# Dealing attention's score pieces by slots of 128 columns, and reading the experts' places three units later

## The chip, the cores and the metric

The kernel runs on one core of one Trainium2 chip. The metric is device time in microseconds of one execution; before the change the median of three runs is 1528.75 us (1524.66 to 1529.18). The profile comes from one further execution of 1526.24 us.

## The reference

Two layers over x of 2 x 2048 tokens with 256 features. What matters here is the attention of the second layer, cut from the reference:

```python
xn = _layernorm(x, axis=-1)
q = heads(xn @ Wq + bq); k = heads(xn @ Wk + bk); v = heads(xn @ Wv + bv)     # 16 heads of 16
slopes = 1.0 / base ** jnp.arange(1, 9)                                        # base = 24 ** (1 / 8)
fwd = slopes * jnp.tril(rel) + jnp.triu(neg, 1)        # heads 0 to 7 look back
bwd = slopes * jnp.triu(-rel) + jnp.tril(neg, -1)      # heads 8 to 15 look ahead
scores = jnp.einsum('bhqd,bhkd->bhqk', q, k) * (1.0 / np.sqrt(hd)) + bias[None]
out = jnp.einsum('bhqk,bhkd->bhqd', softmax(scores), v) ... @ Wf + bf
```

Around it: layer 0 (a gated linear attention and a linear layer with quantised weights), which comes first, and beside and after attention a mixture of 8 experts (hidden size 1024): a Sinkhorn iteration over the router's logits, the two best experts of each token, and their outputs added with their weights.

## The kernel before

The program runs layer 0, then attention, then the experts' blocks. The change touches attention alone, which is lines 1606 to 1980.

**Heads and row groups.** Each head's 16 features are padded to 32 rows, so that four heads fill TensorE's 128 rows. A score matmul uses 32 of them (a row group, `r` 0 to 3), and the four row groups work side by side. `way` is the direction (0 looks back, 1 looks ahead), and each way has two groups of four heads.

**Pieces.** Queries go by tiles of 256 (`QT`), and a step is (batch, way, query tile); a part is a step and one of its groups of heads. For each row group, `pieces_of` (line 1617) lists a part's pieces: one block of 128 keys against up to 256 queries. A piece on the diagonal needs a mask. For a head with a steep slope, far keys weigh nothing, so the outer pieces are narrower: 32, 64, 96 and so on to 256 columns of queries.

**Units.** `_units` (1606) deals the pieces out when the program is built. A unit gives each row group up to 512 columns (`WIDE`), which is one PSUM bank of scores. Pieces are taken in the order of the list; where the next does not fit into what is left of the 512, the largest that fits is taken first, and where none fits a piece is cut. So nearly every unit has exactly 512 columns in every row group, with pieces of any multiple of 32. There are 148 units and 1772 pieces. Their order within a unit goes by the columns that each row group has been given so far (`taken`).

**A unit's work.** `scores` (1825) multiplies each piece, keys as the stationary operand (32 rows x 128 columns), queries as the moving one (line 1831), into the tile `sc`, a PSUM bank for each row group; ScalarE then takes the exponential of each row group's bank into `pt` (line 1837). `keep_only` (1840) cuts the diagonal pieces with a mask, on VectorE, one unit later. `weighted_sums` (1846) multiplies `pt` with the values (128 rows x 32 columns, line 1851) into `o_ps`, two units later (`LATE`). A matmul in full precision is two records of the trace. The `sc` banks come from a pool of six that all small PSUM tiles of the stage share.

**Chores.** Between units stand: the copy of a finished part (`o_sb`), its transposes (`o_tr`, line 1787, and `on_tr`, line 1806) and the output projection (`f_ps`, line 1541); one step of the router (Sinkhorn and the choice of experts) a unit, on VectorE mostly; then the sends of token rows into a table by expert, on GpSimd (line 2208).

**The experts' start.** Counted from the last unit: at 32 (`BEGIN`) the places of the first two blocks are loaded from the table into `at` (line 2257, on SyncE's queue, after all sends) and their weights are gathered on GpSimd. At 14 (`FETCH`) VectorE turns the places into indices and weights (`fetch_rows`, lines 2275 to 2282, three instructions a block), and GpSimd gathers the tokens' rows into `xb` (line 2554, two gathers a block). In the four units after that, one sum each of the first block's weights is formed (`combine`, 2287). At 4 from the end `xb` is transposed (`open_rows`, 2301, into `x_ps`). VectorE's instructions in these functions stand in the order in which they are written.

The order of TensorE's instructions is made by the framework's scheduler from this program; in the built program bursts of scores and bursts of weighted sums alternate, with the chores between.

Of the kernel before, what the change touches and what calls it, by code (L numbers as in the profile page):

```python
# [64 lines left out]
P = 128  # L65
# [14 lines left out]

ORDERS = ((0, 1, 7, 6, 2, 3, 4, 5), (2, 3, 5, 4, 0, 1, 7, 6))
WIDE = 512
CENTER = N // 2
NEG_INF = -1.0e9
NE, FF = 8, 1024
# [14 lines left out]
LIMIT = 16.0  # L100
SHIFT = 48.0
BEGIN = 32
FETCH = 14
LATE = 2
OPEN = 4
KR = HD + 5
# [1499 lines left out]
def _units():  # L1606

    tiles = QT // P

    def pieces_of(way, group, r, qt):


        found = [(qt * 2 + way, 0, QT, P * way), (qt * 2 + 1 - way, P * (1 - way), P, 0)]  # L1620
        slope = _slopes()[PLACES[(2 * way + group) * 4 + r] % (H1 // 2)]
        reach = math.ceil((104 + LIMIT - SHIFT) / slope) + 1
        for j in range(1, tiles * (N // QT - 1 - qt if way else qt) + 1):


            width = min(QT, reach - 1 - P * (j - 1))
            if width > 0:
                width = -(-width // 32) * 32
                kb = qt * tiles + tiles - 1 + j if way else qt * tiles - j
                found.append((kb, QT - width if way else 0, width, None))  # L1630
        return found

    steps = [(b, way, qt) for b in range(B) for way in range(2) for qt in ORDERS[way]]
    parts = [(step, group, n % 2) for n, step in enumerate(steps) for group in range(2)]
    rows = []
    for r in range(4):
        row = deque()
        for n, ((b, way, qt), group, bank) in enumerate(parts):
            row.append((n, deque(pieces_of(way, group, r, qt))))
        rows.append(row)  # L1640
    units = []
    done, begun = [[None] * len(parts) for _ in range(4)], set()
    while any(rows):
        this = len(units)
        left, masks = [deque() for _ in range(4)], []
        for r, row in enumerate(rows):
            at = 0
            while row and at < WIDE:
                n, found = row[0]
                b, way, qt = parts[n][0]  # L1650
                if n >= OPEN and any(d[n - OPEN] is None or d[n - OPEN] == this for d in done):
                    break
                first = (r, n) not in begun
                begun.add((r, n))
                if found[0][0] != qt * 2 + way and found[0][2] > WIDE - at:

                    fits = [m for m, piece in enumerate(found) if piece[2] <= WIDE - at]
                    found.rotate(-max(fits, key=lambda m: found[m][2], default=0))
                kb, q0, width, diagonal = found.popleft()
                now = min(width, WIDE - at)  # L1660
                if now < width:
                    rest = None if diagonal is None else diagonal - now
                    found.appendleft((kb, q0 + now, width - now, rest))
                if not found:
                    done[r][n] = this
                    row.popleft()
                left[r].append((r, *parts[n], kb, q0, q0 + now, at, first, not found))
                if diagonal is not None:
                    m0, m1 = max(diagonal, 0), min(diagonal + P, now)
                    if m0 < m1:  # L1670
                        masks.append((r, parts[n][0][1], at + m0, m1 - m0, m0 - diagonal))
                at += now
        widths = [sum(piece[6] - piece[5] for piece in pieces) for pieces in left]
        taken, pieces = [0] * 4, []
        while any(left):
            r = min((r for r in range(4) if left[r]), key=lambda r: taken[r])
            piece = left[r].popleft()
            taken[r] += piece[6] - piece[5]
            pieces.append(piece)
        ended = [part for n, part in enumerate(parts)  # L1680
                 if all(d[n] is not None for d in done) and max(d[n] for d in done) == this]
        units.append((pieces, widths, masks, ended))
    return units
# [3 lines left out]
def attention(  # L1687
# [137 lines left out]
    def scores(pieces, widths):  # L1825
        pt = p2.tile([P, 4, WIDE], F32, tag="pt", name="pt", bufs=4)
        scs = [ps_m.tile([P, WIDE], F32, tag="mm", name="sc") if width else None for width in widths]
        for r, (b, way, qt), group, bank, kb, q0, q1, at, first, last in pieces:
            rows = slice(r * HR, (r + 1) * HR)
            heads = operands.heads[2 * way + group]  # L1830
            nc.tensor.matmul(  # L1831
                scs[r][:, at : at + q1 - q0], lhsT=heads[rows, 1, kb * P : (kb + 1) * P],
                rhs=heads[rows, 0, qt * QT + q0 : qt * QT + q1], start=True, stop=True,
            )
        for r, width in enumerate(widths):
            if width:
                nc.scalar.activation(pt[:, r, 0:width], scs[r][:, 0:width], AF.Exp)  # L1837
        return pt
# [7 lines left out]
    def weighted_sums(pieces, pt):  # L1846


        for r, (b, way, qt), group, bank, kb, q0, q1, at, first, last in pieces:
# [5 lines left out]
            )  # L1855

    units = _units()

    sums = [ps_o.tile([P, 2 * QT], F32, tag=f"o{n}", name="o_ps") for n in range(2)]
# [84 lines left out]
    for n, (pieces, widths, masks, ended) in enumerate(units):  # L1944
        if n in (len(units) // 4 - 4, len(units) // 4):
            next(bias)
        if n == len(units) - BEGIN:
# [5 lines left out]
            for block in ahead:  # L1953
                block.load_gate_up()
        if n == len(units) - FETCH:
            for block in ahead:
                block.fetch_rows()
        if len(units) - FETCH < n <= len(units) - FETCH + 4:
            ahead[0].combine(0, range(n - len(units) + FETCH - 1, n - len(units) + FETCH))
        pt = scores(pieces, widths)  # L1960
# [668 lines left out]
def _constants():  # L2629
# [15 lines left out]
    c["keepmask"] = np.where(mask == 0, np.float32(3e38), np.float32(0))  # L2645
    c["pos"] = np.stack([np.arange(N) - CENTER, np.ones(N)]).astype(f32)
    sel = np.zeros((P, P), f32)
# [26 lines left out]
def _slopes():  # L2674
    half = H1 // 2
    base = np.float32(24.0 ** (1.0 / half))
    return (np.float32(1.0) / base ** np.arange(1, half + 1, dtype=np.float32)).astype(np.float32)


def _bias_rows():  # L2680
# [3 lines left out]
    low = slopes - high  # L2684
    pos = (np.arange(N) - CENTER).astype(np.float32)
    q, k = np.ones((2, H1, KR - HD, N), np.float32)
# [107 lines left out]
```

## Time and profile before

| what | value |
|---|---|
| median of 3 runs | 1528.75 us (1524.66 to 1529.18) |
| profiled execution | 1526.24 us, span 1524.4 us |
| granted TensorE clock | 0.989 |
| attention, first score to last weighted sum | 430.7 to 842.5 us |
| scores, PE (L1831) | 3544 records, 207.6 us busy |
| weighted sums, PE (L1851) | 3544 records, 163.1 us busy |
| exponentials, ACT (L1837) | 589, 302.8 us busy |
| masks, DVE (`keepmask`) | 568, 121.3 us busy |
| largest terms of the chain | PE h_ps 26%, y_ps 14% (experts); sc 9%, o_ps 7%, f_ps 2% (attention) |

How to read it: busy times are unions, so overlapping instructions of one group count once, while the mean of one counts each whole; PE is the matmul, PEld the weight load beside it. The "idle before" column of a group is the time for which its engine stood still just before these instructions, and what ended that. The share of a window is taken of its length.

### The profile page before, as it was taken

How to read it: one execution, taken by the hardware profiler on the slowest of the kernel's cores; microseconds unless marked ns; L12 is line 12 of the kernel's file. 1: busy time of each engine (PE TensorE's matmuls, PEld its weight loads, DVE VectorE, ACT ScalarE, POOL GpSimd, SP SyncE). 2: the span in 40 equal slices, each digit the busy share in tenths (PEclk: the TensorE clock that was granted, in tenths of full speed). 3: DMA queues.
4: the chain of work that ended last, by engine and by line, in shares of the span. 5: the costliest groups of instructions: out<-in, count | busy, mean ns of one | idle time of the engine just before them, and what ended most of it. 6: DMA issues, size and time to landing. Idle time of an engine off the chain costs nothing.

```text
span 1524.4 us, 35795 instructions
## 1 busy us (share of the span) xinstructions
PE 1466.6 (96%) x14948; PEld 1235.1 (81%) x14948; DVE 1010.1 (66%) x2639; ACT 720.6 (47%) x1400; POOL 539.8 (35%) x449
## 2 busy tenths in 40 slices
PE   7889999999899999999999999999999999999996
PEld 4556766776668888778888799989899998989996
DVE  6787677565458876854356677767666776767663
ACT  5445555454467777767877223323232333223221
POOL 4342222122120000598931144343434544343342
PEclk9999999999999999999999999999999999999998
DMA  7001101410452210340041765575765867666541
GB/s 233 0 14 58 56 30 47 101 57 29 111 135 43 44 49 16 53 85 6 4 183 44 244 211 182 185 254 190 257 234 191 257 197 269 205 220 246 176 100 24
DMA packets 75866, 192.09 MB, mean 126 GB/s; under 512 B 19008, under 2 KB 56640, under 8 KB 63232
## 3 DMA queue, kind: packets, MB, share of 16 engines
q0 software_dynamic: 28256, 144.23, 29.0%
q1 hardware_dynamic: 46336, 44.30, 11.6%
q8 instruction: 120, 1.97, 0.5%
q10 hardware_dynamic: 1104, 1.18, 0.3%
q14 instruction: 50, 0.41, 0.1%
HBM read 157.95 MB, written 32.10 MB: 125 GB/s over the span
## 4 chain that ended last, share of the span: by engine, by line
PE 62%; DVE 2%; issue 0%; ACT 0%; POOL 0%; POOLq 0%; ACTq 0%
PE h_ps L119 26%; PE y_ps L119 14%; PE sc L1831 9%; PE o_ps L1851 7%; PE f_ps L1541 2%; PE h_ps L2477 1%; PE x_ps L119 1%; PE o_tr L1787 1%; DVE pt L119 1%; PE on_tr L1806 0%; PE h_ps L2512 0%; DVE va L119 0%; DVE larger L119 0%; DVE o_sb L119 0%; PE h_ps L2500 0%
## 5 line engine op out<-in xcount | busy, mean ns | idle before, releaser
L1837 ACT ACTIVATE pt<-sc 128x512 f32<-128x512 f32 (+1 forms) x589 | 302.8, 600 | 104.0 <-ACT pt L1837 40.4
L1831 PE MATMUL sc<-qk 32*128 32x256 f32 (+6 forms) x3544 | 207.6, 333 | 3.9 <-issue 2.0
L119 DVE TENSOR_TENSOR larger<-larger,h_ps 128x512 f32<-128x512 f32 x160 | 109.9, 687 | 145.0 <-ACT larger L119 83.6
L1831 PEld LDWEIGHTS sc<-qk 32*128 32x128 f32 x3544 | 176.6, 186 | 33.2 <-issue 18.7
L119 PE MATMUL y_ps<-qk,larger 128*128 128x256 f32 x704 | 173.4, 380 | 0.3 <-DVE larger L119 0.3
L1851 PE MATMUL o_ps<-pt,va 128*32 128x256 f32 (+7 forms) x3544 | 163.1, 312 | 1.8 <-DVE o_sb L119 1.8
L119 ACT COPY larger<-h_ps 128x512 f32<-128x512 f32 x128 | 74.5, 582 | 174.9 <-PE h_ps L119 174.9
L1851 PEld LDWEIGHTS o_ps<-pt,va 128*32 128x32 f32 x3544 | 126.4, 110 | 27.3 <-issue 7.5
L2391 POOL DMA_INDIRECT out<-va,to x64 | 103.9, 1623 | 123.4 <-DVE larger L119 69.7
L119 DVE TENSOR_TENSOR pt<-pt,keepmask 128x128 f32<-128x128 f32 (+3 forms) x568 | 121.3, 272 | 34.3 <-ACT pt L1837 34.0
L2208 POOL DMA_INDIRECT table<-rows,place x64 | 68.0, 1063 | 194.5 <-DVE pt L119 180.2
L119 PEld LDWEIGHTS y_ps<-qk,larger 128*128 128x128 f32 x704 | 124.0, 191 | 12.3 <-DVE larger L119 0.7
L119 PEld LDWEIGHTS h_ps<-va,qk 128*128 128x128 f32 x1024 | 126.6, 192 | 6.7 <-issue 3.1
L119 PE MATMUL h_ps<-va,qk 128*128 128x128 f32 x1024 | 130.6, 276 | 0.3 <-ACT larger L119 0.3
L2554 POOL DMA_INDIRECT xb<-normed,to x64 | 65.6, 1025 | 146.6 <-DVE wt L2282 80.4
L119 ACT ACTIVATE larger<-larger 128x512 f32<-128x512 f32 x64 | 40.4, 632 | 117.8 <-DVE larger L119 117.8
L119 ACT ACTIVATE va<-va 128x512 f32<-128x512 f32 x64 | 40.4, 632 | 103.6 <-DVE va L119 103.3
L119 PE MATMUL y_ps<-larger 128*128 128x256 f32 x320 | 79.0, 380 | 0.0
L119 POOL TENSOR_TENSOR pause<-ones_mat,expo 128x4 f32<-128x4 f32 x64 | 68.5, 1071 | 2.0
L119 ACT COPY va<-h_ps 128x512 f32<-128x512 f32 x64 | 36.9, 576 | 56.2 <-PE h_ps L119 56.2
L119 PE MATMUL h_ps<-larger,qk 128*128 128x128 f32 x512 | 62.8, 276 | 0.0
L119 PEld LDWEIGHTS h_ps<-larger,qk 128*128 128x128 f32 x512 | 59.7, 192 | 2.5 <-issue 2.5
(322 smaller groups left out, 2840.7 us busy)
## 6 DMA issues: line engine op xcount, KB each, us to landing
qk<-qk SPq DMA_DIRECT2D x32, 256.0 KB
qk<-qk SPq DMA_DIRECT2D x64, 128.0 KB
va<-v SPq DMA_DIRECT2D x4, 1208.0 KB
v<-v SPq DMA_DIRECT2D x8, 574.0 KB
normed<-xn SPq DMA_DIRECT2D x8, 512.0 KB
out<-acc SPq DMA_DIRECT2D x8, 512.0 KB
acc<-in_x SPq DMA_DIRECT2D x7, 512.0 KB
table<-rows,place POOLq DMA_INDIRECT x64, 3.0
```

Of the source, the lines that this page charges most:

```text
L119: return lambda *a, **k: self.tc.keep_in_program_order(begin(*a, **k))
L1541: multiply(out[r : r + HR], left[:, r : r + HR], *args, **how)
L1787: nc.tensor.transpose(ps[:, n, :], o_sb[:, n * P : (n + 1) * P], ident)
L1831: nc.tensor.matmul(scs[r][:, at : at + q1 - q0], lhsT=heads[rows, 1, kb * P : (kb + 1) * P], rhs=heads[rows, 0, qt * QT + q0 : qt * QT + q ...
L1837: nc.scalar.activation(pt[:, r, 0:width], scs[r][:, 0:width], AF.Exp)
L1851: nc.tensor.matmul(sums[bank][r * HR : (r + 1) * HR, to + q0 : to + q1], lhsT=values[b, way][:, kb, h * VC : h * VC + HR], rhs=pt[:, r, at ...
L2208: send = self.tc.keep_in_program_order(self.nc.gpsimd.indirect_dma_start(out=self.c.table, in_=self.rows[:, t, :], in_offset=None, out_off ...
L2391: send = e.nc.gpsimd.indirect_dma_start(out=e.out, in_=y[:, c, :], in_offset=None, out_offset=bass.IndirectOffsetOnAxis(ap=self.to[:, c : ...
L2477: self.e.nc.tensor.matmul(ps[rows, :], lhsT=self.xT[:, c * P + r * SB : c * P + (r + 1) * SB], rhs=self.w[:, r, at : at + ST], start=c == ...
L2554: self.nc.gpsimd.indirect_dma_start(out=to, out_offset=None, in_=self.c.normed, in_offset=bass.IndirectOffsetOnAxis(ap=at, axis=0),)
```

## The change

Two things are altered.

A unit's row group still holds at most 512 columns, and now also at most 576 slots (`SLOTS`), where a piece counts as its columns, and as 128 at least. `part` is what could be cut off a piece here, a multiple of 128. A part's first (diagonal) piece is taken whole if it fits and cut to `part` if not. Of the other pieces the widest that fits is taken; if none fits, the widest that leaves 128 columns or more behind after a cut at `part` is cut; if there is none of these either, the row group's share of this unit ends there, short of 512. The order within a unit goes by slots. The built program has 150 units and 1505 pieces with the same 299,520 columns, 512 masks (all 128 columns wide) in place of 568, and 598 exponentials in place of 589.

`FETCH` goes from 14 to 11: the places are read, the rows gathered and the first block's sums begun 11 units before the end. `open_rows` stays at 4. The order of all instructions on GpSimd is the same as before; on SyncE's queue a few loads of the second batch's keys stand together that were in two lots.

```diff
+SLOTS = 576
...
-FETCH = 14
+FETCH = 11
...
-            at = 0
+            at = slots = 0
             while row and at < WIDE:
                 n, found = row[0]
                 b, way, qt = parts[n][0]
                 if n >= OPEN and any(d[n - OPEN] is None or d[n - OPEN] == this for d in done):
                     break
                 first = (r, n) not in begun
+
+                def fits(width):
+                    return width <= WIDE - at and max(P, width) <= SLOTS - slots
+
+                part = min(WIDE - at, SLOTS - slots) // P * P
+                if found[0][0] == qt * 2 + way:
+                    m, now = 0, found[0][2] if fits(found[0][2]) else part
+                else:
+                    whole = [m for m, piece in enumerate(found) if fits(piece[2])]
+                    wide = whole or [m for m, piece in enumerate(found) if piece[2] - part >= P]
+                    if not wide:
+                        break
+                    m = max(wide, key=lambda m: found[m][2])
+                    now = found[m][2] if whole else part
+                if not now:
+                    break
                 begun.add((r, n))
-                if found[0][0] != qt * 2 + way and found[0][2] > WIDE - at:
-
-                    fits = [m for m, piece in enumerate(found) if piece[2] <= WIDE - at]
-                    found.rotate(-max(fits, key=lambda m: found[m][2], default=0))
+                found.rotate(-m)
                 kb, q0, width, diagonal = found.popleft()
-                now = min(width, WIDE - at)
...
-                at += now
+                at, slots = at + now, slots + max(P, now)
...
-            taken[r] += piece[6] - piece[5]
+            taken[r] += max(P, piece[6] - piece[5])
```

## The prediction

> **What bounds the kernel now.** I read the page first, then the busy time of the attention stage alone, then single bursts of it on the timeline, and last the waits.
>
> ```profile
> span 1524.4 us, 35795 instructions
> ...
> PE 1466.6 (96%) x14948; PEld 1235.1 (81%) x14948; DVE 1010.1 (66%) x2639; ACT 720.6 (47%) x1400; POOL 539.8 (35%) x449
> ...
> PE   7889999999899999999999999999999999999996
> ```
>
> TensorE is busy everywhere. The change touches only attention, so I cut that stage out by the first and last instruction of the scores (L1831) and the weighted sums (L1851): 430.7 to 842.5 us, 411.8 us for 148 units, 2.78 us each.
>
> ```profile
> 431.00:843.00 412.00, 406.62 (x7896) 338.72 (x7894) 271.11 (x1014) 303.73 (x591) 155.23 (x142) 0.99 0.26 61
> ```
>
> The columns are length, PE, weight loads, DVE, ACT, POOL. PE idles 5 us of 412; ACT has 108 us free and DVE 141. Whatever shortens PE's work here shortens the stage, until ACT or DVE is in the way. What PE's work costs is seen on the timeline (start, length, what, how many):
>
> ```profile
> 709.09 1.15 PE L1831 MATMUL sc<-qk 32*128 32x224 f32 x20
> 710.17 1.07 PE L1851 MATMUL o_ps<-pt,va 128*32 128x224 f32 x24
> 711.07 1.04 PE L1541 MATMUL f_ps<-cwf,onT 128*32 128x256 f32 x16
> 712.04 1.52 PE L1831 MATMUL sc<-qk 32*128 32x96 f32 x30
> 713.49 1.07 PE L1851 MATMUL o_ps<-pt,va 128*32 128x224 f32 x24
> ```
>
> A unit is one burst of scores and one of weighted sums; each piece is two PE records. Both score bursts fill all four row groups with 512 columns each. The first has pieces of 128 columns and more (10 pieces), the second has 15, in one row group 64, 128, 256, 32 and 32; it takes 0.37 us longer. The weighted sums take 1.07 us in both. The groups of instructions by shape say why:
>
> ```profile
> L1831 PEld LDWEIGHTS sc<-qk 32*128 32x128 f32 x3541 | 176.4, 186 | 31.9 <-issue 17.3 <-ACT pt L1837 6.6 <-DVE o_sb L119 2.5
> L1851 PEld LDWEIGHTS o_ps<-pt,va 128*32 128x32 f32 x3544 | 126.4, 110 | 27.3 <-issue 7.5 <-DVE o_sb L119 2.9 <-DVE pi L119 0.9
> ```
>
> ```profile
> L1831 PE MATMUL sc<-qk 32*128 32x256 f32 x1318 | 165.7, 399 | 2.1 <-PE norm_ps L535 1.1 <-issue 1.0
> L1831 PE MATMUL sc<-qk 32*128 32x128 f32 x1044 | 130.8, 293 | 1.9 <-issue 1.0 <-ACT pt L1837 0.9
> L1831 PE MATMUL sc<-qk 32*128 32x32 f32 x344 | 43.1, 241 | 0.0
> L1831 PE MATMUL sc<-qk 32*128 32x96 f32 x182 | 37.8, 298 | 0.0
> L1851 PE MATMUL o_ps<-pt,va 128*32 128x128 f32 x1044 | 113.5, 279 | 0.3 <-DVE o_sb L119 0.2
> L1851 PE MATMUL o_ps<-pt,va 128*32 128x96 f32 x182 | 30.2, 255 | 0.0
> ```
>
> A score piece loads 128 key columns as weights whatever its queries (186 ns); a weighted sum loads 32 (110 ns). So a score record of 96 columns is no shorter than one of 128 (298 against 293 ns), while a weighted sum gets shorter (255 against 279).
>
> To price this I took every run of score matmuls in the trace, from its start to that of the next PE work, and set it against its slots: the largest, over the four row groups, of the sum of max(128, columns). Medians: 512 slots 1.09 us (21 bursts), 544 1.21 (15), 576 1.17 (11), 608 1.17 (20), 640 1.28 (34), 672 1.30 (22), 704 1.41 (7), 768 1.51 (12), 800 1.91 (3), and one of 128 slots 0.42. From 512 to 768 that is 0.42 us for 256 slots, 1.64 ns a slot.
>
> **Scores.** The same 299,520 columns were 1772 pieces in 148 units and become 1505 in 150: of 32 columns 172 become 76, of 64 86 become 4, of 96 91 become none. Bursts, in the program order of each kernel: before 147 (the first holds three units), after 149: the first again, 79 of 512 slots, 63 of 544, 4 of 576, one of 384 and one of 256. Slots summed over bursts fall from 92,160 to 79,200.
> Before, without the first burst, the medians times the counts give 183.5 us of the 192.9 us that these bursts took; the other 9.4 us are waits. After: 79 x 1.09 + 63 x 1.205 + 4 x 1.172 + 1.5 for the last two = 168.2 us. That is 15.3 us less, with the 9.4 us of waits left as they are. The bounds: if a 544 burst is worth what the line through 512 and 768 says (1.14 us) the gain is 19.4 us; if the waits double, it is 5.9. I take 15.3, because the 544 row is measured.
>
> **Weighted sums.** Two more units are two more bursts: 151.6 us over 148 units is 1.02 us each, +2.0 us. Their largest column sums grow only by 768 (76,160 to 76,928), which is one and a half full bursts, +1.5; I take +2.0.
>
> **ACT.** Exponentials rise from 589 to 598 with the same columns. A 128-column one takes 277 ns and a 512 one 603, so an instruction's fixed part is some 0.17 us: +1.5 us of ACT's 304, beside PE. Back to back four of them take 2.06 us (pitch 0.48 us), against PE's shortest unit, 1.09 + 1.02 = 2.11 us. It fits, just: I take 0; the bound on the loss is in the rivals.
>
> **DVE.** Masks fall from 568 to 512, all 128 wide. The 128-wide row gives 107.7 us for 456, 0.236 each: 120.9 us after, against some 132 now. The chain puts 2.2% of the stage (9 us) on these masks, so a gain up to 9 us is conceivable; but the crowds of masks at the unit where a batch half begins (12 in the first, 9 to 12 near 626 us) remain at 10 to 12, so I take 0. In the units up to 76, where the router's steps run, DVE is busy 2.1 to 2.6 us of each unit of 2.5 to 3.0; with 0.1 to 0.2 us less per unit it is tighter, and that is the loss bound.
>
> **Places read 11 units from the end.** What moves is, per block of two, three small DVE instructions (0.16 to 0.21 us), two gathers on POOL, and behind them four DVE sums of 0.68 us in the four units that follow. In order:
>
> ```profile
> 776.60 1.22 SPq L2257 DMA_DIRECT2D at<-table  x2
> ```
>
> ```profile
> 802.54 0.16 DVE L2275 CAST to<-at 128x2 int32<-128x2 f32 x1
> ```
>
> ```profile
> 802.97 0.95 POOL L2554 DMA_INDIRECT xb<-normed,to  x1 [23.88 <-DVE wt L2282]
> ```
>
> The places are loaded 25 us before DVE reads them, so reading later saves no wait. The last of four gathers starts at 806.74 and lands 4.2 us later, 8.4 us after the read. The transposes that need it (x_ps) run at 830.8 us, ten units on. After, seven units of some 2.6 us leave 18 us for 8.4: still hidden. Behind the gathers POOL only waits for the keys' tiles (next gather at 834.97). Cost 0; at worst the four sums (2.7 us) collide with the 19 masks of units 144 and 145.
>
> **Sum**, against the profiled execution's 1526.24 us: -15.3 + 2.0 = -13.3, 1512.9 us; I say 1513. That execution lies 2.5 us under the median of the three (1528.75), inside their spread of 4.5. What a measurement here can tell from no change is 0.3%, 4.6 us.
>
> **Rivals.**
> - *Waits take part of the gain.* ACT frees a PSUM bank every 0.48 us; six banks serve four per unit, so the third and fourth row group of a burst wait for the first two exponentials of the one before: they end about 0.96 us after that burst, and the next starts 1.02 us after it. For it: that margin, and DVE's 2.6 us in the router's units. Against: ACT waits show as 6.6 us now, and the 21 bursts of 512 slots, under the same condition, have the 1.09 us that I use. If the 9.4 us of waits double: 1522. Chance 0.15.
> - *The floor is lower than 128 columns.* For it: the 32-column records of the scores are shorter than the 128-column ones (241 against 293 ns). Were the floor 64 columns, the largest sums would go from 79,648 to 76,928, -2720 x 1.64 ns = -4.5, and with +2.0 for two units the time would be 1523.7. Against it: the two bursts above would then differ by 64 columns, 0.1 us, and differ by 0.37; and 96 columns cost what 128 do. Chance 0.08. The Trainium skill's page "TensorEngine Tiling (Array Packing)", section "Instruction Overhead", speaks for this rival: it puts the overhead of a matmul at some 60 cycles, so that a free size of 1 lasts as long as one of 60. By that, as an estimate, the sum would be -1.7 us; the score records of 96 and 128 columns do not agree with it.
> - *Slower: a unit has its price whatever is in it.* If ACT's round (2.06 us and its semaphores), not PE's, sets the pace once the scores are shorter, shorter bursts become waits and two more units cost 2 x 2.78 = 5.6 us: 1531.8. It decides from the point where ACT's round exceeds PE's 2.11 us. Against: ACT is free 26% of the stage, and units now differ with their slots. Chance 0.08.
> - *The later read stalls the first block.* It needs a landing 18 us after the read; 8.4 was seen. With 5 us lost: 1518. Chance 0.03.
>
> **How the numbers follow.** The main case (1508 to 1518) has 0.66. Faster by over 0.3% is all of it, 0.13 of the waits' case and the late read's 0.03: 0.82. Within 0.3%: the rest of the waits' case and the floor's, 0.10. Slower: 0.08. The range goes from the upper bound of the gain (-19.4 + 1.5, and 3 of the masks' 9 us: 1505) to the waits' case with the 2.5 us by which the median lies over the profiled run, 1524.
>
> **What would show it.** Right: score bursts that fall from 1.36 us (200.3 over 147) to 1.24 (184.9 over 149), weighted sums at 1.07, a stage of some 398 us, PE busy 98%, the same length after it. Wrong: gaps before L1845's loads put down to ACT or to masks that grow past 15 us, score bursts of 544 slots at 1.3 us, or idle PE before x_ps.

## The result and the profile after

The changed kernel takes 1515.26 us (median of four runs, 1512.88 to 1516.36) against 1527.2 us of the kernel before beside it. The ratio is 0.9921 with a 95% interval of 0.9899 to 0.9942: 12 us faster, 9 to 15. The profiled execution is 1514.98 us, 11.3 us under the 1526.24 us of the one before. Lines move: the scores are now L1845, their exponentials L1851, the weighted sums L1865, the records of the helper L120.

The page of the changed kernel:

```profile
span 1512.9 us, 33605 instructions
...
PE 1456.4 (96%) x13880; PEld 1194.7 (79%) x13880; DVE 1005.6 (66%) x2583; ACT 720.8 (48%) x1409; POOL 543.1 (36%) x449
...
L1845 PE MATMUL sc<-qk 32*128 32x256 f32 (+3 forms) x3010 | 195.8, 356 | 1.7 <-PE norm_ps L536 1.1
L1845 PEld LDWEIGHTS sc<-qk 32*128 32x128 f32 x3010 | 152.3, 187 | 37.6 <-issue 19.1
...
L1865 PE MATMUL o_ps<-pt,va 128*32 128x256 f32 (+3 forms) x3010 | 163.3, 338 | 2.8 <-DVE o_sb L120 2.6
```

The scores' busy time falls from 207.6 to 195.8 us; the weighted sums stay where they were (163.1 and 163.3), with 15% fewer pieces. The attention stage, first score to last weighted sum, now goes from 431.9 to 830.7 us: 398.9 us in place of 411.8. Busy times of about that stretch (length, PE, weight loads, DVE, ACT, POOL):

```profile
431.00:831.00 400.00, 394.65 (x6827) 296.43 (x6827) 267.62 (x961) 303.79 (x600) 158.28 (x142) 0.99 0.25 61
```

PE is busy 98.7% of it, as before. Outside the stage the two executions differ by 1.7 us the other way; the changed one has a stretch of half clock just ahead of the stage that the other does not have (last section).

Cut into bursts as in the prediction, start of a run of scores to the start of the next work: 200.3 us before, 185.9 after, 14.4 less; everything else in the stage (weighted sums and chores) 211.5 before, 213.0 after, 1.5 more. Bursts on the timeline of the changed kernel:

```profile
696.69 1.20 PE L1845 MATMUL sc<-qk 32*128 32x256 f32 x24
697.82 1.08 PE L1865 MATMUL o_ps<-pt,va 128*32 128x256 f32 x18
...
702.42 1.15 PE L1845 MATMUL sc<-qk 32*128 32x128 f32 x20
703.51 1.07 PE L1865 MATMUL o_ps<-pt,va 128*32 128x256 f32 x23
```

Score bursts of over 1.4 us, the first aside, fall from 36 of 146 to 12 of 148; a weighted sum's burst is 1.07 us as ever.

What TensorE's weight loads waited for, in the attention stage of the kernel before:

```profile
PEld sc L1831 <- issue: 18.7, 60, 1.4
PEld o_ps L1851 <- issue: 7.5, 29, 0.8
PEld sc L1831 <- ACT pt L1837: 6.6, 29, 0.8
...
PEld o_tr L1787 <- ACT pt L1837: 1.6, 7, 0.4
```

and of the changed one:

```profile
PEld sc L1845 <- issue: 19.1, 74, 1.3
PEld o_ps L1865 <- issue: 15.2, 50, 0.9
PEld sc L1845 <- ACT pt L1851: 11.3, 46, 0.8
PEld o_tr L1801 <- ACT pt L1851: 5.5, 18, 0.4
```

More waits are put down to ScalarE. Whether that is a new bound is one question for the experiments. The others: is it the floor of 128 columns that was paid, or the number of pieces; which half of the new dealing brings the gain; and does the later read do anything. Times on different chips are compared by their ratio to the kernel before on the same chip. One per cent is 15.3 us.

### The profile page after: what moved, and what is told of

The parts are those of the page before. It is cut to its first block, busy times and chain, and to the rows that moved or that the text cites. A ratio compares the mean times of both kernels' runs of the same rounds, so it can differ in the third digit from the quotient of the medians.

```text
span 1512.9 us, 33605 instructions
## 1 busy us (share of the span) xinstructions
PE 1456.4 (96%) x13880; PEld 1194.7 (79%) x13880; DVE 1005.6 (66%) x2583; ACT 720.8 (48%) x1409; POOL 543.1 (36%) x449
## 3 DMA queue, kind: packets, MB, share of 16 engines
q10 hardware_dynamic: 1104, 1.18, 0.2%
## 4 chain that ended last, share of the span: by engine, by line
PE 62%; DVE 2%; issue 0%; ACT 0%; POOL 0%; POOLq 0%; DVEq 0%; ACTq 0%
PE h_ps L120 26%; PE y_ps L120 15%; PE sc L1845 9%; PE o_ps L1865 7%; PE f_ps L1542 2%; PE h_ps L2491 1%; PE o_tr L1801 1%; PE x_ps L120 1%; PE h_ps L2526 0%; PE on_tr L1820 0%; DVE pt L120 0%; DVE larger L120 0%; DVE va L120 0%; PE h_ps L2514 0%; DVE onT L120 0%
## 5 line engine op out<-in xcount | busy, mean ns | idle before, releaser
L1851 ACT ACTIVATE pt<-sc 128x512 f32<-128x512 f32 (+1 forms) x598 | 302.9, 594 | 90.8 <-ACT pt L1851 37.7
L120 DVE TENSOR_TENSOR larger<-larger,h_ps 128x512 f32<-128x512 f32 x160 | 110.0, 687 | 145.6 <-ACT larger L120 84.3
L1845 PE MATMUL sc<-qk 32*128 32x256 f32 (+3 forms) x3010 | 195.8, 356 | 1.7 <-PE norm_ps L536 1.1
L1845 PEld LDWEIGHTS sc<-qk 32*128 32x128 f32 x3010 | 152.3, 187 | 37.6 <-issue 19.1
L120 PE MATMUL y_ps<-qk,larger 128*128 128x256 f32 x704 | 173.4, 380 | 0.3 <-DVE larger L120 0.3
L1865 PE MATMUL o_ps<-pt,va 128*32 128x256 f32 (+3 forms) x3010 | 163.3, 338 | 2.8 <-DVE o_sb L120 2.6
L120 ACT COPY larger<-h_ps 128x512 f32<-128x512 f32 x128 | 74.5, 582 | 175.1 <-PE h_ps L120 175.1
L1865 PEld LDWEIGHTS o_ps<-pt,va 128*32 128x32 f32 x3010 | 101.8, 110 | 47.4 <-issue 15.2
L120 DVE TENSOR_TENSOR pt<-pt,keepmask 128x128 f32<-128x128 f32 x512 | 115.9, 285 | 28.3 <-ACT pt L1851 27.7
L120 PEld LDWEIGHTS y_ps<-qk,larger 128*128 128x128 f32 x704 | 124.1, 191 | 12.2 <-DVE larger L120 0.7
L120 PEld LDWEIGHTS h_ps<-va,qk 128*128 128x128 f32 x1024 | 126.7, 192 | 6.7 <-issue 3.1
L120 PE MATMUL h_ps<-va,qk 128*128 128x128 f32 x1024 | 130.6, 276 | 0.3 <-ACT larger L120 0.3
L120 ACT ACTIVATE larger<-larger 128x512 f32<-128x512 f32 x64 | 40.4, 632 | 117.8 <-DVE larger L120 117.8
L120 ACT ACTIVATE va<-va 128x512 f32<-128x512 f32 x64 | 40.4, 632 | 103.6 <-DVE va L120 103.3
L120 PE MATMUL y_ps<-larger 128*128 128x256 f32 x320 | 79.0, 380 | 0.0
L120 POOL TENSOR_TENSOR pause<-ones_mat,expo 128x4 f32<-128x4 f32 x64 | 70.0, 1094 | 2.0
L120 ACT COPY va<-h_ps 128x512 f32<-128x512 f32 x64 | 36.9, 576 | 56.2 <-PE h_ps L120 56.2
L120 PE MATMUL h_ps<-larger,qk 128*128 128x128 f32 x512 | 62.8, 276 | 0.0
L120 PEld LDWEIGHTS h_ps<-larger,qk 128*128 128x128 f32 x512 | 59.7, 192 | 2.5 <-issue 2.5
```

What stands on the lines that cost most here:

```text
L120: return lambda *a, **k: self.tc.keep_in_program_order(begin(*a, **k))
L1845: nc.tensor.matmul(scs[r][:, at : at + q1 - q0], lhsT=heads[rows, 1, kb * P : (kb + 1) * P], rhs=heads[rows, 0, qt * QT + q0 : qt * QT + q ...
L1865: nc.tensor.matmul(sums[bank][r * HR : (r + 1) * HR, to + q0 : to + q1], lhsT=values[b, way][:, kb, h * VC : h * VC + HR], rhs=pt[:, r, at ...
```

## Experiments: what a narrow piece costs

In `scores` alone, each piece of 256 columns is multiplied in two parts. The dealing, the exponentials and the weighted sums stay.

```diff
+            cuts = (0, 128, QT) if q1 - q0 == QT else (0, q1 - q0)
+            for c0, c1 in zip(cuts, cuts[1:]):
-                scs[r][:, at : at + q1 - q0], ...
+                    scs[r][:, at + c0 : at + c1], ...
```

> The changed kernel, in which each of the 871 score pieces of 256 columns is multiplied as two of 128, so 2376 pieces in place of 1505, with the same slots (78,976 summed over the units' largest row groups). Slots of 128 set the price: no more than 5 us longer than the changed kernel's 1515 us, score bursts at about 1.25 us on average as now. The number of pieces sets it (the 267 pieces that the change saved then cost some 14 us, 52 ns each): 871 x 0.052 = 45 us longer, 1560 us.

Measured 1526.1 us, ratio 0.9989 (0.9975 to 1.0003). The changed kernel on this chip (with the read 14 units from the end, see below) has 0.9912, so 871 more pieces of no more slots cost 0.77%, 11.8 us, or 13.5 ns a piece (the intervals of the two ratios leave 10 to 17). Neither theory had that: pieces have a small price, a quarter of the 52 ns that would explain the change by their number. A burst of that kernel, now with 32 records:

```profile
741.79 1.29 PE L1847 MATMUL sc<-qk 32*128 32x128 f32 x32
743.01 1.07 PE L1867 MATMUL o_ps<-pt,va 128*32 128x256 f32 x16
```

From its start to that of the weighted sums it takes 1.22 us, which is also the median of that kernel's bursts; the median of the changed kernel's is 1.15.

The same with `(0, 224, QT)`:

> The same, but cut into 224 and 32 columns: the same 2376 pieces and columns as the cut at 128, only the slots differ. Sum over units of the largest row group by the floor of a piece: 104,096 at 128 (25,120 more than now), 94,880 at 96 (18,080 more), 85,760 at 64 (9,088 more), no more at 32. At 1.64 ns a slot: floor 128 gives 41 us over the changed kernel (1556 us), floor 96 gives 30 us (1545), floor 64 gives 15 us (1530), no floor gives the time of the cut at 128. The number of pieces alone: the same as the cut at 128.

Measured 1551.33 us, ratio 1.0142 (1.0123 to 1.0161): 1.53%, 23.4 us more than the cut at 128, with the same pieces. The floor is there, but the price is short of the 41 us of full slots. Two bursts of that kernel:

```profile
741.79 1.62 PE L1847 MATMUL sc<-qk 32*128 32x128 f32 x32
743.34 1.07 PE L1867 MATMUL o_ps<-pt,va 128*32 128x256 f32 x20
744.34 1.44 PE L1847 MATMUL sc<-qk 32*128 32x224 f32 x32
745.70 1.08 PE L1867 MATMUL o_ps<-pt,va 128*32 128x256 f32 x20
```

Almost all its bursts have 704 slots. By the line of the prediction they should last 1.09 + 192 x 1.64 ns = 1.40 us and a little for the pieces; the median is 1.37. Against 1.22 us for the cut at 128 that is 0.15 us, which is 96 slots, not 192. There are two ways to read this: the floor is at some 80 columns for every piece, or it is 128 and one of the two narrow pieces of a row group is paid while the other is not. In 224, 32, 224, 32 the last one has nothing behind it. So the order was turned, `(0, 32, QT)`, which a floor of 80 would not notice:

> As the cut into 224 and 32 columns, but 32 first, then 224: the same pieces and the same slots (104,448 over the bursts). Plain slots: the same time as that one, 1551 us. If a narrow piece costs a full slot only when another piece of its row group follows it in the burst (the last one's columns alone count), the cut at 224 has 91,232 such columns and this has 104,448: 13,216 x 1.64 ns = 22 us longer, 1573 us, score bursts of two halves at about 1.52 us against 1.37.

Measured 1563.71 us, ratio 1.0241 (1.0224 to 1.0258), and the bursts have a median of 1.53 us:

```profile
741.04 1.61 PE L1847 MATMUL sc<-qk 32*128 32x32 f32 x32
742.58 1.07 PE L1867 MATMUL o_ps<-pt,va 128*32 128x256 f32 x18
743.58 1.61 PE L1847 MATMUL sc<-qk 32*128 32x128 f32 x32
```

A start-to-start of 1.54 us (741.04 to 742.58) where the prediction of this run had 1.52. So a narrow piece costs 128 columns when another piece of its row group follows in the burst, and its own columns when none does. The changed kernel's own bursts of 544 slots say the same: in 27 of the 63 the account comes to 512 columns, because the narrow piece stands last, and these have a median of 1.09 us; the other 36 have 1.18.

Why this is so, no run shows. The Trainium skill's page "TensorE: Matmul & The Clock Gate", section "Step-by-step: what each phase is for", says that the weights of the next matmul are loaded while the present one runs. A load that lasts longer than the matmul it hides behind would look like this, and these runs agree with it. So do the weighted sums, whose weights have 32 columns: in the kernel before their bursts have a median of 1.00 us, start to start, with 20 records and of 1.02 with 30. But they use other rows of TensorE too, so this does not decide it.

The sum fell short: 1.0%, 15 us, in place of 22, since a quarter of the bursts of the kernel cut at 224 lasted over 1.5 us too. Half of these, 20 of 40, stand behind a step of the router (`sk_ps`); such bursts have a median of 1.74 us in that kernel and 1.78 in this one, so there the added columns vanish in a wait that was there anyway. What it is a wait for is open.

With this account (all pieces of a row group but the last at 128 at least, the last at its own columns, largest row group of each burst) the kernel before has 84,704 columns and the changed one 78,208: 6496 x 1.64 ns = 10.7 us, and 267 pieces x 13.5 ns = 3.6 us. Together 14.3, where 14.4 were measured. That they agree so closely is luck: the price of a piece is known to 10 to 17 ns only, and it was measured in bursts of 16 pieces.

If order alone helps, a row group's narrowest piece should come last:

```diff
-        for r, (b, way, qt), group, bank, kb, q0, q1, at, first, last in pieces:
+        for r, (b, way, qt), group, bank, kb, q0, q1, at, first, last in narrow_last(pieces):
             rows = slice(r * HR, (r + 1) * HR)
```

> The changed kernel, in which each row group's narrowest score piece of a unit is multiplied last; the weighted sums keep their order. If only a narrow piece with another behind it costs a slot, the columns that count fall from 78,208 to 76,928: 2.1 us less than the changed kernel's 1515 us. Plain slots: no difference.

Measured 1514.99 us, ratio 0.9908 (0.9888 to 0.9927). The times do not tell it from the changed kernel. In the profile the bursts of 544 slots fall from a median of 1.15 to 1.11 us and the stage by 1.1 us (397.8), half of what was expected.

## Experiment: which half of the dealing

The widest piece that fits is still taken first, but cuts may be anywhere and there is no limit of slots:

```diff
-                    return width <= WIDE - at and max(P, width) <= SLOTS - slots
+                    return width <= WIDE - at
-                part = min(WIDE - at, SLOTS - slots) // P * P
+                part = WIDE - at
-                    wide = whole or [m for m, piece in enumerate(found) if piece[2] - part >= P]
+                    wide = whole or list(range(len(found)))
```

> The changed kernel without its limit of slots and with cuts at any column: the widest piece that fits first, and each row group filled to 512 columns. 148 units, 1631 pieces, slots 91,136 (before 92,160, changed 78,976). Slots: 1024 slots less than before, -1.7 us, so about 1525 us, and all but that of the change's gain is gone. The number of pieces: 141 of the 267 saved, half of the gain, 1520 us. If the gain came from the order of the pieces (widest first) it stays at 1515.

Measured 1522.37 us, ratio 0.9964 (0.9946 to 0.9981), between the first two expectations and 8 us above the changed kernel on the same chip (0.9912). So cutting at 128s, with the limit of slots, is the larger part of the gain. By the account above this kernel has 1120 columns and 141 pieces less than before, 3.7 us; 5.5 were measured, with an interval of 2.9 to 8.3. In its profiled execution (1519.02 us, the fastest of the six) a part of the gain is the clock and not the dealing (last section); whether that holds for the median is not shown.

## Experiment: the later read

```diff
-FETCH = 11
+FETCH = 14
```

> The changed kernel with the places read 14 units from the end again. The later read costs and brings nothing (forecast): the same as the changed kernel within 2 us, 1513 to 1517. If the earlier read of places makes VectorE wait for the sends now that the units are shorter: idle VectorE before the read of the places and a longer time, by what is seen there; the slack seen was 25 us.

Measured 1515.5 us, ratio 0.9912 (0.9895 to 0.9928), against the changed kernel's 0.9921; the attention stage is 398.9 us in both. No effect of the read is seen either way. In the changed kernel the places are loaded at

```profile
770.60 0.88 SPq L2271 DMA_DIRECT2D at<-table  x2
```

read 30.6 us later,

```profile
801.16 0.16 DVE L2289 CAST to<-at 128x2 int32<-128x2 f32 x1
```

and the last gather is issued at

```profile
805.38 0.95 POOL L2568 DMA_INDIRECT xb<-normed,to  x1 [0.30 <-issue]
```

The transposes of `xb` stand at 820.4 us, 19 us after the read, and no wait is shown ahead of them but 0.2 us for ScalarE.

## Experiments: is ScalarE the new bound

One more exponential in each unit, of numbers that are of no use, first in the changed kernel, then in the one before:

```diff
+        nc.scalar.activation(idle, c.ones_mat, AF.Exp)
         return pt
```

> The changed kernel with one more exponential of 128 x 128 numbers in each unit, whose result nobody reads (150 on ScalarE, some 0.2 to 0.3 us each, 30 to 42 us of its 303 in the stage). If ScalarE's release of the score banks now holds TensorE back (the waits put down to it rose from 6.6 to 11.3 us at the score loads), the time grows by 5 us or more, and by more than the kernel before grows under the same addition. If ScalarE is beside the path, by less than 3 us.

> The kernel before with the same exponential added in each of its 148 units. With more free time between its exponentials it should grow by less than the changed kernel does under the same addition: 0 to 4 us, 1529 to 1533. If both grow alike, the shorter score bursts did not bring ScalarE closer to the path.

Measured 1552.33 (ratio 1.0158) and 1562.26 us (1.0223), 37 and 34 us more than without. That would have been ScalarE on the path in both kernels, but the runs don't show it. The additions depend on nothing, and the scheduler put all of them (150 and 148) among the exponentials of the first 16 units (not 30, as an expectation below has it); here the kernel before:

```profile
448.11 3.40 ACT L1838 ACTIVATE idle<-ones_mat 128x128 f32<-128x128 f32 x10
451.42 2.04 ACT L1837 ACTIVATE pt<-sc 128x512 f32<-128x512 f32 x4
453.32 3.74 ACT L1838 ACTIVATE idle<-ones_mat 128x128 f32<-128x128 f32 x11
```

Ten exponentials in a row in each unit hold up any kernel. And not all of the 37 and 34 us is ScalarE's own: from 430 to 515 us the granted clock was 0.74 and 0.72, against 0.96 in the kernels without the addition. The two were repeated with all exponentials held in the order in which they are written:

```diff
+    scalar = InOrder(tc, nc.scalar)
-                nc.scalar.activation(pt[:, r, 0:width], scs[r][:, 0:width], AF.Exp)
+                scalar.activation(pt[:, r, 0:width], scs[r][:, 0:width], AF.Exp)
+        scalar.activation(idle, c.ones_mat, AF.Exp)
```

> The changed kernel with one more exponential of 128 x 128 numbers behind the four of each unit, now held in that place (before, the scheduler had drawn all of them into the first 30 units, where they took 34 to 37 us in a row in both kernels). One took 0.31 us, so ScalarE's round of a unit goes from 2.06 to some 2.4 us. TensorE's shortest round is 1.09 + 1.02 = 2.11 in the changed kernel. If ScalarE is as near to the path as that, units without chores lose up to 0.3 us each: 10 to 35 us in all, and more than the kernel before loses. If ScalarE has room, under 3 us.

> The kernel before with the same exponential held behind the four of each unit. Its units without chores last 2.2 to 2.5 us (score bursts of 1.17 to 1.51 and 1.02), so a round of 2.4 us on ScalarE costs part of them 0.1 to 0.2 us: 3 to 12 us, clearly less than in the changed kernel. Growth alike in both would say that the shorter bursts brought ScalarE no closer.

Measured 1514.48 us, ratio 0.9905 (0.9888 to 0.9921), and 1530.01 us, ratio 1.0003 (0.9993 to 1.0012). Nothing in either kernel. The stage of the changed kernel with the addition:

```profile
431.00:831.00 400.00, 394.25 (x6851) 296.41 (x6849) 268.48 (x963) 331.17 (x754) 160.23 (x142) 1.00 0.26 64
```

ScalarE is busy 27 us longer (331.2 against 303.8), and TensorE's time does not move. Each addition stands behind the four of its unit, and in 91 of 150 cases a pause of over 0.15 us follows, as here:

```profile
702.56 2.07 ACT L120 ACTIVATE pt<-sc 128x512 f32<-128x512 f32 x4 [0.69 <-PE sc L1845]
704.49 0.33 ACT L120 ACTIVATE idle<-ones_mat 128x128 f32<-128x128 f32 x1
705.47 2.01 ACT L120 ACTIVATE pt<-sc 128x512 f32<-128x512 f32 x4 [0.65 <-PE sc L1845]
```

So here ScalarE waits for the scores, not the other way round, and its rate is not what the waits with its name are about. The last test frees one bank of four without it, that of the fourth row group, from unit 89 on, where VectorE has time:

```diff
+        if direct and widths[3]:
+            vector.tensor_copy(pt[:, 3, 0 : widths[3]], scs[3][:, 0 : widths[3]])
...
+                src = pt[:, r, 0:width] if direct and r == 3 else scs[r][:, 0:width]
+                nc.scalar.activation(pt[:, r, 0:width], src, AF.Exp)
```

> The changed kernel, in which from unit 89 on VectorE copies the fourth row group's scores out of PSUM and ScalarE takes their exponential in SBUF, so that this bank is free before ScalarE comes to it. If the waits put down to ScalarE at the score loads and the transposes (11.3 and 5.5 us) are waits for banks, the 61 units lose up to half of them: 3 to 6 us less than the changed kernel, 1509 to 1512. If they are something else: no gain, or a loss where the masks stand behind the copies of 0.7 us on VectorE.

Measured 1516.7 us, ratio 0.9916 (0.9899 to 0.9932); stage 399.9 us. The waits at the score loads with ScalarE's name fall from 11.3 to 8.7 us, and those for VectorE's work on `pt` (masks and now copies) rise from 1.4 to 3.5. No gain: in the changed kernel, moving the fourth bank's release off ScalarE is worth nothing. It is a weak test. By the prediction's account the next burst waits for the banks of the first two row groups, and these were left with ScalarE; that their release holds TensorE back is not excluded.

## Experiment: the two small gains together

```diff
+    scalar = InOrder(tc, nc.scalar)
...
-        for r, (b, way, qt), group, bank, kb, q0, q1, at, first, last in pieces:
+        for r, (b, way, qt), group, bank, kb, q0, q1, at, first, last in narrow_last(pieces):
```

> The changed kernel with each row group's narrowest score piece last, and with the exponentials held in the program's order (as in the run with the added exponential, whose attention stage was 395.4 us against the changed kernel's 398.9 in spite of the addition). The first is worth 1.1 us by the stage of the run that has it alone. If the order of the exponentials is worth the other 3.5 us, the stage falls to some 394 us and the time to 1510.5 us; if those 3.5 us were chance, the stage is 398 us and the time 1514.

Measured 1534.11 us against 1542.2 us of the kernel before on this chip, ratio 0.9942 (0.9925 to 0.9960). The ratio is no better than the changed kernel's, so no gain of the order is seen; but neither expectation came true, and the run can't settle it. On this chip the kernel before is some 14 us slower than on the others, and the stage of this one is 413.7 us, 14.8 more than the changed kernel's. The 3.5 us have another explanation: where the stage with the addition was shorter, TensorE's clock had been full at its start (last section).

In the profile of this run, while the weight gathers that begin at 772 us are under way, TensorE stands still several times for what the profile calls issue (it shows nothing that was waited for), and then has half the clock (the third and second last columns of the windows are clock and DMA share):

```profile
775.78 0.43 PE L1878 MATMUL o_ps<-pt,va 128*32 128x256 f32 x6 [0.81 <-issue]
777.24 0.29 PE L1878 MATMUL o_ps<-pt,va 128*32 128x128 f32 x1 [1.02 <-issue]
```

```profile
774.10:777.50 3.40, 1.46 (x16) 0.49 (x14) 0.00 (x0) 0.14 (x1) 1.69 (x2) 1.00 1.03 372
777.50:784.30 6.80, 6.80 (x61) 5.38 (x60) 1.97 (x7) 4.14 (x9) 0.00 (x0) 0.50 1.02 429
```

In the changed kernel's profile the gathers fill the DMA engines as much, and TensorE is busy throughout at full clock:

```profile
775.00:785.00 10.00, 10.00 (x188) 7.39 (x186) 6.22 (x23) 6.83 (x14) 0.00 (x0) 1.00 1.00 421
```

What the 14 us of this chip are stays open: the kernel before was not profiled on it.

## Why the prediction was right

- **The stage's bound.** That shortening TensorE's work in attention shortens the stage as much: right. The stage was forecast at some 398 us and took 398.9.
- **Scores, -15.3.** Measured -14.4. The mechanism was right in the main (narrow pieces paid as 128, unless they stand last); that the size came out so well was luck. The medians at 512 and 544 slots were taken as 1.09 and 1.205 us; both are 1.15. That is 79 x 0.06 = 4.7 us more and 63 x 0.055 = 3.5 us less, two errors that nearly cancel. At 544, 27 of the 63 bursts have the narrow piece last and count 512 columns. At 512 the time goes with what stands ahead of a burst: behind a chore (`o_tr`, `on_tr`, `f_ps`) the median is 1.09 us in both kernels, directly behind weighted sums it is 1.15 before and 1.17 after, behind a router step 1.45 and 1.38. These last two kinds are 10 of the 21 bursts before and 43 of the 79 after, so the median jumps. The 21 were not "under the same condition".
- **Waits left as they are.** By the prediction's own measure, what the bursts took over their medians, 9.4 us became 8.6; but the median at 512 slots holds waits itself. Taking for each number of slots the value that a tenth of its bursts stay under, the bursts of the kernel before (without the first) lie some 17 us above that in sum, those of the changed one just under 20. So the waits did not double; that they grew by some 2 us rests on the second measure alone.
- **Pieces.** Their price, 13.5 ns each in the run that cuts at 128, is no term of the prediction; its medians by slots hold it unseen, since bursts of more slots also have more pieces.
- **Weighted sums, +2.0.** With the chores, +1.5.
- **ACT, 0.** Right, and with more room than the prediction gave it. It set four exponentials of 2.06 us against a round of 2.11; the run with 0.33 us more work for ScalarE in each unit, and no more time, says that the margin is larger.
- **DVE, 0.** Masks fell to 115.9 us (120.9 forecast). The "some 132" of the prediction adds up the widths one by one, which overlap; together they took 121.3 before, so the fall is 5.4 us and not 11. Their share of the stage's chain went from 2.2 to 1.6%, 9 to 6 us, inside the bound given.
- **The later read, 0.** Right; 18 us were forecast between the read and the transposes, 19 were seen.
- **The rivals.** The floor below 128 columns: refuted as put, since 32 columns with a piece behind them cost 96 more; the pure rule of 128 was not right either. The overhead of some 60 cycles that the Trainium skill's page "TensorEngine Tiling (Array Packing)", section "Instruction Overhead", states is not the floor of these score matmuls. A price for each unit whatever is in it: refuted, two units more and 12 us less. Waits that take part of the gain: some 2 us at most.

## What to carry to other kernels

In these matmuls, which use a quarter of the rows and load 128 columns of weights for each piece, a piece narrower than 128 is paid as 128, unless it is the last of its row group in the burst. So deal such work in lots of 128, even at the price of bins that are not quite full. Putting what is narrow last took 1.1 us off the stage in a profile, which the times could not tell from nothing. A median by slots hides what stands ahead of a burst; before it is multiplied by a new count, ask whether the new bursts stand where the old ones did. And before a rising wait is taken for a new bound, give the engine that it names more work: here 9% more on ScalarE cost nothing.

## What was not expected of the hardware

**A halved clock at the start of attention.** The first burst of the stage was 7.33 us before and 7.44 after, and the prediction left it out of its sum. The clock is a part of it: where the clock stays full, it is 5.76 us (cuts anywhere) and 5.80 (added exponentials in order). The granted clock falls to half for 6.8 us in both, here in windows of 3.4 us around it, before:

```profile
430.00:433.40 3.40, 2.10 (x34) 1.75 (x34) 1.94 (x8) 1.66 (x4) 0.00 (x0) 1.00 0.51 178
433.40:436.80 3.40, 3.15 (x34) 2.77 (x38) 3.40 (x17) 2.74 (x6) 2.89 (x1) 0.51 0.55 139
436.80:440.20 3.40, 3.40 (x44) 2.15 (x40) 0.82 (x4) 2.21 (x5) 3.40 (x2) 0.50 0.93 259
```

and after:

```profile
430.50:433.90 3.40, 1.80 (x32) 1.36 (x28) 1.61 (x4) 1.34 (x4) 0.00 (x0) 1.00 0.49 173
433.90:437.30 3.40, 3.31 (x25) 2.68 (x27) 3.33 (x16) 2.64 (x7) 2.29 (x1) 0.50 0.38 86
```

TensorE was not idle in the stretch ahead of the fall; it was busy 2.10 and 1.80 of 3.40 us. The changed kernel has a fall a little earlier too (first line, busy 1.38 us ahead of it); the kernel before, busy 1.70, has none there (the other two):

```profile
416.80:420.20 3.40, 3.17 (x10) 2.07 (x10) 0.69 (x1) 1.35 (x3) 0.00 (x0) 0.50 1.03 365
413.00:416.40 3.40, 1.70 (x8) 0.71 (x7) 1.60 (x7) 2.67 (x6) 0.46 (x1) 1.00 0.17 58
416.40:419.80 3.40, 2.62 (x12) 1.54 (x12) 0.69 (x1) 1.57 (x3) 0.00 (x0) 1.00 1.02 361
```

In the kernel with cuts anywhere, the clock stays full there:

```profile
433.00:440.00 7.00, 6.57 (x108) 4.89 (x108) 6.13 (x26) 6.72 (x14) 5.36 (x2) 1.00 0.68 184
```

and so it does in the run with the added exponentials held in place (full from 425 to 448 us). Half of 6.8 us is 3.4 us of work, about what its stage of 395.4 us is shorter by; its fall came ahead of the stage instead (416.9 to 423.7 us), so the execution as a whole does not gain these. The Trainium skill's page "TensorE: Matmul & The Clock Gate", section "What's actually happening", has a monitor that judges by windows of 3413 ns and halves the clock after an idle one. The length of the stretches agrees (3.4, 6.8 and 10.2 us in these traces). An idle window was not needed: ones that were 53 and 62% busy were followed by a fall. The busy share alone does not decide either, since the one of 50% above was not; what does is open. So the stages of two kernels that differ by 3.5 us may differ in the clock alone.
